# Reordering the normalisation and the stores at the end of a fused attention and FFN layer

## The chip, the cores and the metric

The kernel runs on one core of one Trainium2 chip. The metric is the device time of a run in microseconds (us). The core has a matrix engine (TensorE, "PE" in the profile, with its weight loads as "PEld"), a vector engine (VectorE, "DVE"), a scalar engine with function tables (ScalarE, "ACT"), a general engine (GpSimd, "POOL") and a queue engine (SyncE, "SP"). Each engine runs its own instructions in order; semaphores order them against each other. DMA transfers can be issued by SP, by ScalarE and by GpSimd.

## The reference

The input is `x`, 4 x 2048 tokens of 256 features in float32. Two sublayers follow each other, each with a residual and a layer norm:

```python
x = layernorm(x + attn(x))     # attn: S = (Q K^T) * decay mask, in chunks of 32 tokens; O = S V
                               # attn(x) = (sigmoid(x W_g^T) * O) W_o^T + x
x = layernorm(x + ffn(x))      # ffn: silu(x wg^T) * (x wu^T), times wd^T, hidden size 768
```

The FFN weights are integers from -127 to 127 with a scale of 1/127. `layernorm` subtracts the mean over the 256 features and divides by the root of variance + 1e-5; it has no gain and no bias.

## The kernel before, in words

The 8192 tokens are cut into 16 blocks of 512 (`TB`), and each block into four groups of 128 tokens (`NG`), one token per partition. A loop over `b` from 0 to 13 overlaps the FFN of block `b` with the attention of block `b + 2`; one iteration takes 32 us. Blocks 14 and 15 have their FFN after the loop, in the tail. Three products in the attention are done with seven multiplications instead of eight (`seven`), with sums made on GpSimd. The FFN multiplies activations split in a high part and an fp16 rest (`u_hi`, `u_lo`).

The program is written with a tile framework: it inserts the semaphores, hands out the buffers of each pool in turn (the eight PSUM banks by `bank`), and chooses the order of each engine's instructions from a planner's priorities and costs. An instruction may so run much earlier than it is written. Where `in_turn` (that is, `tc.keep_in_program_order`) is wrapped around an instruction, it keeps its written place among all instructions so wrapped.

The FFN keeps the integer weights exact only up to 128 in size. So the kernel looks at the weights' largest values (`look_up`, one piece at the end of each of the first six iterations, 0.94 us on VectorE), counts how many are too large (`count_wide`: a comparison `wide` on VectorE, a matmul of one row `pw`, a sum and a cast on VectorE to `n_wide`), and reads that count at the very end. If it isn't zero, everything is done again in float32 (`wide_block`); with these inputs it is zero, and the branch costs only the reading of `n_wide` on each engine (L929) and the jump (L932).

The tail is what the change is about. `ffn_up` (L646) multiplies up for block 15 in two halves of 256 tokens, `ffn_down` makes `r_before`, the residual of block 14, and `moments` (L290, `bn_stats` at L295 and `bn_aggr` at L296) its mean and variance in `mv_before`. After `count_wide` (L801), `root` (L299) has ScalarE take the square root `std_before`. That changes ScalarE's function table[...]. Then a loop over the four groups of block 15 does for each group `g`:

- 12 matmuls (L853) and the residual `r[:, g, :]` on VectorE (L861), then its moments (L295, L296);
- for `g == 0`, `normalize` of all of block 14: reciprocal (L806) and rescale (L809) on VectorE, four shifts, minus mean times reciprocal, on GpSimd (L815), four scalings on ScalarE (L824), and then one store of 512 KB from SP (L691);
- the root of this group on ScalarE (L304);
- for `g` 1 and 2, `normalize_first`: the oldest waiting group is normalised in the same way and stored, 128 KB from SP (L838). At `g == 2` it is called twice.

Group 3 is then normalised on VectorE alone (L876, L877) and stored. Because of `in_turn`, the reciprocal for a group stands in VectorE's order at the place where `normalize` is called.

Of the kernel before, what the change touches and what calls it, by code (L numbers as in the profile page):

```python
# [47 lines left out]
F32 = mybir.dt.float32  # L48
# [3 lines left out]
AF = mybir.ActivationFunctionType  # L52
ALU = mybir.AluOpType

P = 128
# [3 lines left out]
TB = 512  # L59
NG = TB // P  # L60
# [3 lines left out]
H_UP = 2.0**23  # L64
# [6 lines left out]
def kernel(  # L71
# [15 lines left out]
    nc = tc.nc  # L87
    NT, D = x.shape
# [1 line left out]
    KD = D // P  # L90
    KH = H // P
    NB = NT // TB
    assert NB > 3

    const = ctx.enter_context(tc.tile_pool(name="const", bufs=1))
    setup = ctx.enter_context(tc.tile_pool(name="setup", bufs=2))
# [1 line left out]
    work = ctx.enter_context(tc.tile_pool(name="work", bufs=2))  # L98
# [6 lines left out]
    small = ctx.enter_context(tc.tile_pool(name="small", bufs=8))  # L105
    psum = ctx.enter_context(tc.tile_pool(name="psum", bufs=8, space=bass.MemoryType.PSUM))

    def bank(name):
        return psum.tile([P, TB], F32, tag="ps", name=name)


    def span(b, start):
        return slice(b * TB, (b + 1) * TB) if start is None else bass.ds(start, TB)
# [142 lines left out]
    top = const.tile([P, 6], F32, tag="top", name="top")  # L256

    def look_up(i):
        w = (fg, fu, fd)[i // 2][0].bitcast(F32)
        half = w.shape[1] // 2  # L260
        reduced = nc.vector.tensor_reduce(
            top[:, i : i + 1],
            w[:, i % 2 * half : (i % 2 + 1) * half, :].rearrange("p k n -> p (k n)"),
            mybir.AxisListType.X,
            ALU.max,
            apply_absolute_value=True,
        )
        tc.keep_in_program_order(reduced)

    def count_wide():  # L270

        wide = const.tile([P, top.shape[1]], F32, tag="wide", name="wide")
        nc.vector.tensor_scalar(wide, top, EXACT, None, ALU.is_gt)
        ones = const.tile([P, 1], F32, tag="ones", name="ones")
        nc.vector.memset(ones, 1.0)
        pw = bank("pw")
        nc.tensor.matmul(pw[:1, : top.shape[1]], lhsT=ones, rhs=wide, start=True, stop=True)
        count = const.tile([1, 1], F32, tag="count", name="count")
        nc.vector.tensor_reduce(count, pw[:1, : top.shape[1]], mybir.AxisListType.X, ALU.add)
        n_wide = const.tile([1, 1], I32, tag="n_wide", name="n_wide")  # L280
        nc.vector.tensor_copy(n_wide, count)
        return n_wide

    def in_turn(ins):
        tc.keep_in_program_order(ins)
# [4 lines left out]
    def moments(r, name, groups=range(NG), order=free):  # L290

        mv = small.tile([P, NG, 2], F32, tag="mv", name=f"mv_{name}")
        for g in groups:
            st = small.tile([P, 6], F32, tag="st", name=f"st_{name}_{g}")
            order(nc.vector.bn_stats(st, r[:, g, :]))  # L295
            order(nc.vector.bn_aggr(mv[:, g, :], st))  # L296
        return mv

    def root(mv, name, on_r=1.0, groups=range(NG), order=free):  # L299

        std = small.tile([P, NG], F32, tag="rstd", name=f"rstd_{name}")
        span = slice(groups[0], groups[-1] + 1)
        order(
            nc.scalar.activation(  # L304
                std[:, span], mv[:, span, 1], AF.Sqrt, bias=eps, scale=1 / on_r**2
            )
        )
        return std
# [236 lines left out]
    def back_terms(g, parts, ws):  # L545


        pairs = list(zip(parts, ws))[:: -1 if g % 2 else 1]
        return [term for part, w in pairs for term in zip(part, w)]
# [128 lines left out]
    def ffn_down(b, uT, h):  # L678
        r = work.tile([P, NG, D], F32, tag="r2", name=f"r2_{b}")

        def residual(gs, pb):

            nc.vector.scalar_tensor_tensor(
                flat(r, gs), pb, SCALE**3 / U_UP * H_UP, flat(h, gs), ALU.mult, ALU.add
            )

        project_back(b, uT, [chunked(w) for w in fd], residual, "fdn")
        return r

    def store(b, r, start=None):  # L690
        nc.sync.dma_start(  # L691
            out[span(b, start), :].rearrange("(g p) d -> p g d", p=P), r
        )
# [38 lines left out]
    looked = 0  # L732

    for b in range(NB - 2):
# [38 lines left out]
        r = ffn_down(b, uT, hs.pop(b))  # L773
# [3 lines left out]
        if looked < top.shape[1]:  # L777
            look_up(looked)
            looked += 1
    for i in range(looked, top.shape[1]):  # L780
        look_up(i)

# [2 lines left out]
    last = NB - 1  # L787
    per = NG // 2
    cols = [slice(i * per * P, (i + 1) * per * P) for i in range(2)]
# [7 lines left out]
    r_before = ffn_down(last - 1, uT, hs[last - 1])  # L797
    mv_before = moments(r_before, f"f{last - 1}")
    ffn_up(last, hTs[last], uT_last, range(len(early), KH), cols[0])
    ffn_up(last, hTs[last], uT_last, range(KH), cols[1])  # L800
    n_wide = count_wide()  # L801

    def normalize(r, mv, rstd, name, on_r=1.0, groups=range(NG)):

        span = slice(groups[0], groups[-1] + 1)
        in_turn(nc.vector.reciprocal(rstd[:, span], rstd[:, span]))  # L806
        if on_r != 1:
            in_turn(
                nc.vector.tensor_scalar(  # L809
                    rstd[:, span], rstd[:, span], 1 / on_r, None, ALU.mult  # L810
                )
            )
        shift = small.tile([P, NG], F32, tag="shift", name=f"shift_{name}")
        for g in groups:
            nc.gpsimd.tensor_scalar(  # L815
                shift[:, g : g + 1],
                mv[:, g, 0:1],
                rstd[:, g : g + 1],
                -1.0,
                ALU.mult,  # L820
                ALU.mult,
            )
        for g in groups:
            scaled = nc.scalar.activation(  # L824
                r[:, g, :],
                r[:, g, :],
                AF.Identity,
                bias=shift[:, g : g + 1],
                scale=rstd[:, g : g + 1],
            )  # L830
            in_turn(scaled)

    std_before = root(mv_before, f"f{last - 1}", H_UP, order=in_turn)
    r = work.tile([P, NG, D], F32, tag="r2", name=f"r2_{last}")

    def store_group(g):
        tokens = slice(last * TB + g * P, last * TB + (g + 1) * P)
        nc.sync.dma_start(out[tokens, :], r[:, g, :])  # L838

    waiting = []

    def normalize_first():
        g, mv, std = waiting.pop(0)
        normalize(r, mv, std, f"f{last}_{g}", groups=[g])
        store_group(g)

    for g in range(NG):
        pb = bank(f"fdn_{last}_{g}")[:, :D]  # L850
        terms = back_terms(g, uT_last, map(chunked, fd))
        for i, (part, w) in enumerate(terms):
            nc.tensor.matmul(  # L853
                pb,
                lhsT=part[:, g * P : (g + 1) * P],
                rhs=w,
                start=(i == 0),
                stop=(i == len(terms) - 1),
            )
        in_turn(  # L860
            nc.vector.scalar_tensor_tensor(  # L861
                r[:, g, :], pb, SCALE**3 / U_UP, hs[last][:, g, :], ALU.mult, ALU.add
            )
        )
        mv = moments(r, f"f{last}_{g}", [g], order=in_turn)
        if g == 0:
            normalize(r_before, mv_before, std_before, f"f{last - 1}", H_UP)
            store(last - 1, r_before)
        std = root(mv, f"f{last}_{g}", groups=[g], order=in_turn)
        waiting.append((g, mv, std))  # L870
        if 0 < g < NG - 1:
            normalize_first()
        if g == NG - 2:
            normalize_first()
    g, mv, std = waiting.pop()
    in_turn(nc.vector.reciprocal(std[:, g : g + 1], std[:, g : g + 1]))  # L876
    nc.vector.tensor_scalar(  # L877
        r[:, g, :], r[:, g, :], mv[:, g, 0:1], std[:, g : g + 1], ALU.subtract, ALU.mult
    )
    store_group(g)  # L880


    def wide_block(start, weights):
# [46 lines left out]
        n_wide, min_val=0, max_val=top.shape[1] * P, skip_runtime_bounds_check_because="a count"  # L930
# [63 lines left out]
```

## Time and profile before

| | us |
|---|---|
| median of 3 runs | 536.26 (535.37 to 536.46) |
| the profiled execution's own time | 535.63 |
| its span | 533.9 |
| last matmul begins, last VectorE instruction ends | 524.1, 528.99 |
| last store issued | 529.3 |

The span is what the profile covers of the execution; the 1.73 us between it and the execution's own time lie around it. In the profile's rows, "128x256 f32<-128x256 f32 x4" are output and input shapes (partitions x elements) and the count; a bracket at a row's end tells how long the engine sat idle before it and which instruction released it. "L824" is a line of the kernel. All times in the tail are from the start of the span. The mean granted TensorE clock is 0.995.

### The profile page before, as it was taken

The page shows a single profiled execution, that of the slowest core. Times are in us where ns is not written, and L with a number is a line of the kernel's source. Part 1 is how long each engine was busy: PE and PEld are TensorE (multiplying, and loading weights), DVE is VectorE, ACT ScalarE, POOL GpSimd, SP SyncE. Part 2 cuts the span into 40 slices and gives each one's busy share as a digit, 9 for nine tenths or more (in the row PEclk, how much of TensorE's full clock was granted, in tenths as well). Part 3 has the DMA queues.
Part 4 walks back from the last instruction along what each step waited for, and adds up shares of the span by engine and source line. Part 5 has one row for each costly group of instructions (what it writes and reads, how often), then busy time and mean ns, then how long its engine had stood idle before and what let it go on. Part 6 is the DMA issues. An engine that isn't in the chain of part 4 may idle for free.

```text
span 533.9 us, 9939 instructions
## 1 busy us (share of the span) xinstructions
PE 522.8 (98%) x3486; PEld 421.0 (79%) x3486; DVE 391.2 (73%) x1026; ACT 310.8 (58%) x561; POOL 268.4 (50%) x305
## 2 busy tenths in 40 slices
PE   8999999999999999999999999999999999999992
PEld 5688887888878788887888878788887888868792
DVE  4468659587695867859587695867859587698883
ACT  2284556555564754656555664764657566566754
POOL 5132672735636365572735636374572736433651
PEclk9999999999999999999999999999999999999997
DMA  7531312214130231412214130231412113020102
GB/s 253 181 120 39 80 40 69 52 41 119 42 101 18 52 108 41 114 46 63 58 39 120 41 105 15 54 107 40 112 49 78 42 43 78 1 65 16 40 2 82
DMA packets 43126, 36.87 MB, mean 69 GB/s; under 512 B 4673, under 2 KB 38977, under 8 KB 43073
## 3 DMA queue, kind: packets, MB, share of 16 engines
q1 hardware_dynamic: 41952, 35.15, 23.3%
q10 hardware_dynamic: 1088, 1.05, 0.6%
q8 instruction: 29, 0.48, 0.4%
q14 instruction: 25, 0.20, 0.1%
q0 software_dynamic: 32, 0.00, 0.0%
HBM read 20.45 MB, written 8.39 MB: 54 GB/s over the span
## 4 chain that ended last, share of the span: by engine, by line
PE 95%; DVE 2%; ACT 1%; issue 0%; DVEq 0%; POOL 0%
PE fg L656 16%; PE fdn L561 16%; PE fu L656 15%; PE pa L561 10%; PE p_v L379 8%; PE p_y L363 8%; PE p_g L363 8%; PE po L535 5%; PE ps L514 3%; PE pg L459 1%; PE py L475 1%; PE pv L494 1%; PE pi L177 1%; DVE u L668 1%; DVE s L666 1%
## 5 line engine op out<-in xcount | busy, mean ns | idle before, releaser
L676 POOL TENSOR_TENSOR u_lo<-u,u_hi 128x512 f16<-128x512 f32 (+1 forms) x102 | 123.7, 1214 | 144.3 <-ACT u_hi L675 143.8
L666 DVE SCALAR_TENSOR_TENSOR s<-fg,s 128x512 f32<-128x512 f32 (+1 forms) x102 | 66.4, 651 | 48.1 <-ACT s L664 47.6
L664 ACT ACTIVATE s<-fg 128x512 f32<-128x512 f32 (+1 forms) x102 | 58.2, 571 | 66.6 <-PE fg L656 65.9
L675 ACT CAST u_hi<-u 128x512 fp32r<-128x512 f32 (+1 forms) x102 | 60.4, 592 | 31.5 <-DVE u L668 30.7
L656 PE MATMUL fg<-hT_hi,fg_hi 128*128 128x512 f32 (+1 forms) x204 | 74.0, 443 | 0.0
L668 DVE TENSOR_TENSOR u<-fu,s 128x512 f32<-128x512 f32 (+1 forms) x102 | 66.1, 650 | 5.0 <-POOL u_lo L676 1.0
L656 PE MATMUL fu<-hT_hi,fu_hi 128*128 128x512 f32 (+1 forms) x204 | 61.6, 382 | 0.0
L656 PE MATMUL fg<-hT_lo,fg_lo 128*128 128x512 f16 (+1 forms) x204 | 58.9, 370 | 0.0
L656 PE MATMUL fu<-hT_lo,fu_lo 128*128 128x512 f16 (+1 forms) x204 | 58.1, 366 | 0.0
L561 PE MATMUL pa<-wo,goT 128*128 128x256 f32 x256 | 58.0, 379 | 0.0
L561 PE MATMUL fdn<-fd_hi,u_hi 128*128 128x256 f32 x360 | 55.4, 296 | 0.0
L561 PEld LDWEIGHTS pa<-wo,goT 128*128 128x128 f32 x256 | 48.6, 190 | 6.7
L640 POOL TENSOR_TENSOR hT_lo<-hT,hT_hi 128x512 f16<-128x512 f32 x28 | 35.4, 1286 | 28.5 <-ACT hT_hi L639 28.5
L561 PEld LDWEIGHTS fdn<-fd_hi,u_hi 128*128 128x128 f32 x360 | 46.8, 189 | 1.1
L561 PE MATMUL fdn<-fd_lo,u_lo 128*128 128x256 f16 x360 | 44.7, 274 | 0.0
L656 PEld LDWEIGHTS fu<-hT_hi,fu_hi 128*128 128x128 f32 x204 | 37.5, 188 | 7.7
L656 PEld LDWEIGHTS fg<-hT_hi,fg_hi 128*128 128x128 f32 x204 | 35.7, 189 | 8.5
L304 ACT ACT_TABLE_LOAD x30 | 38.5, 1283 | 0.5
L656 PEld LDWEIGHTS <-fu_lo 128*128 128x128 f16 x204 | 20.0, 98 | 21.5 <-DVE sT L524 1.2
L561 PEld LDWEIGHTS <-u_lo 128*128 128x128 f16 x360 | 32.7, 98 | 5.1 <-POOL u_lo L676 0.3
L582 DVE SCALAR_TENSOR_TENSOR h<-x,pa 128x512 f32<-128x512 f32 x32 | 22.0, 688 | 17.5 <-PE pa L561 16.9
L535 PE MATMUL po<-sT,v 128*128 128x128 f32 x256 | 31.2, 275 | 0.0
(150 smaller groups left out, 983.7 us busy)
## 6 DMA issues: line engine op xcount, KB each, us to landing
x<-in_x_dram SPq DMA_DIRECT2D x16, 512.0 KB, 3.4
xT<-in_xT_dram SPq DMA_DIRECT2D x15, 512.0 KB, 4.4
out_dram<-r SPq DMA_DIRECT2D x15, 512.0 KB, 5.1
hT<-sq SPq DMA_DIRECT2D x224, 32.0 KB, 1.9
fg_int<-in_ffn_gT_dram SPq DMA_DIRECT2D x3, 256.0 KB, 8.1
fu_int<-in_ffn_uT_dram SPq DMA_DIRECT2D x3, 256.0 KB, 6.5
fd_int<-in_ffn_dT_dram SPq DMA_DIRECT2D x3, 256.0 KB, 6.0
xT<-in_xT_dram SPq DMA_DIRECT2D x2, 256.0 KB, 3.8
```

Source lines behind the costliest of these rows:

```text
L304: nc.scalar.activation(std[:, span], mv[:, span, 1], AF.Sqrt, bias=eps, scale=1 / on_r**2)
L363: nc.tensor.matmul(pb, lhsT=a[i - 1], rhs=b[i - 1], start=first, stop=True, skip_group_check=True,)
L379: nc.tensor.matmul(pb[:, g * P : (g + 1) * P], lhsT=b[i - 1][:, g * P : (g + 1) * P], rhs=a[i - 1], start=first and g == 0, stop=True, ski ...
L535: nc.tensor.matmul(po[:, cols], lhsT=v[:, g, dc * P : (dc + 1) * P], rhs=sT[:, cols], start=True, stop=True,)
L561: nc.tensor.matmul(pb[:, j * D : (j + 1) * D], lhsT=part[:, g * P : (g + 1) * P], rhs=w, start=(i == 0), stop=(i == len(terms) - 1),)
L640: nc.gpsimd.tensor_tensor(in_order[1], whole, in_order[0].bitcast(F32), ALU.subtract)
L656: nc.tensor.matmul(pb, lhsT=w[kind][:, dc, hc * P : (hc + 1) * P], rhs=hT[kind][:, dc, cols], start=(kind == kinds[0] and dc == 0), stop=( ...
L664: nc.scalar.activation(s, pg, AF.Sigmoid, scale=SCALE / H_UP)
L666: nc.vector.scalar_tensor_tensor(s, pg, U_UP / H_UP**2, s, ALU.mult, ALU.mult)
L668: nc.vector.tensor_tensor(u, pu, s, ALU.mult)
L675: nc.scalar.copy(hi, u)
L676: nc.gpsimd.tensor_tensor(lo, u, hi.bitcast(F32), ALU.subtract)
```

## The change

What is scaled where, and in which order it is stored, changes in the tail:

- `count_wide` is called in iteration 6 of the loop instead of in the tail.
- The reciprocals of block 14 and of group 0 of block 15 stand behind the moments of group 1; those of group 1 behind the moments of group 2; those of groups 2 and 3 at the end.
- Block 14: groups 0 and 1 are scaled by ScalarE, 2 and 3 by GpSimd. Its four shifts become one product for all groups (`shift_before`), with minus the mean computed ahead (`minus_mean`). Four stores of 128 KB take the place of the one of 512 KB: groups 0 and 2 from SP, 1 and 3 from ScalarE's queue.
- Block 15: groups 0 and 1 are scaled by ScalarE (shift 0 on GpSimd, shift 1 on VectorE), groups 2 and 3 by VectorE.
- Stores are in turn as well.

```diff
         if looked < top.shape[1]:
             look_up(looked)
             looked += 1
-    for i in range(looked, top.shape[1]):
-        look_up(i)
+        elif looked == b:
+            n_wide = count_wide()
...
-    n_wide = count_wide()
...
+    def inverse(std, cols, on_r=1.0):
+        in_turn(nc.vector.reciprocal(std[:, cols], std[:, cols]))
         if on_r != 1:
...
+                nc.vector.tensor_scalar(std[:, cols], std[:, cols], 1 / on_r, None, ALU.mult)
...
+    def by_vector(eng, r, g, mv, std):
+
+        in_turn(
+            eng.tensor_scalar(
                 r[:, g, :],
                 r[:, g, :],
+                mv[:, g, 0:1],
+                std[:, g : g + 1],
+                ALU.subtract,
+                ALU.mult,
+            )
+        )
+
+    def by_scalar(r, g, std, shift):
+        scaled = nc.scalar.activation(
+            r[:, g, :], r[:, g, :], AF.Identity, bias=shift, scale=std[:, g : g + 1]
+        )
+        in_turn(scaled)
+
+    def shift_of(eng, g, mv, std):
+        shift = small.tile([P, 1], F32, tag="shift_last", name=f"shift_{last}_{g}")
+        in_turn(
+            eng.tensor_scalar(
+                shift, mv[:, g, 0:1], std[:, g : g + 1], -1.0, ALU.mult, ALU.mult
+            )
+        )
+        return shift
...
+    minus_mean = small.tile([P, NG], F32, tag="minus", name=f"minus_{before}")
+    nc.vector.tensor_scalar(minus_mean, mv_before[:, :, 0], -1.0, None, ALU.mult)
+    shift_before = small.tile([P, NG], F32, tag="minus", name=f"shift_{before}")
+    of_group = []
     for g in range(NG):
...
         mv = moments(r, f"f{last}_{g}", [g], order=in_turn)
         if g == 0:
-            normalize(r_before, mv_before, std_before, f"f{last - 1}", H_UP)
-            store(last - 1, r_before)
-        std = root(mv, f"f{last}_{g}", groups=[g], order=in_turn)
-        waiting.append((g, mv, std))
-        if 0 < g < NG - 1:
-            normalize_first()
-        if g == NG - 2:
-            normalize_first()
...
+            std_before = root(mv_before, f"f{before}", H_UP, order=in_turn)
+        of_group.append((mv, root(mv, f"f{last}_{g}", groups=[g], order=in_turn)))
+        if g == 1:
+            inverse(std_before, slice(0, NG), H_UP)
+            mv, std = of_group[0]
+            inverse(std, slice(0, 1))
+            shift = shift_of(nc.gpsimd, 0, mv, std)
+            in_turn(
+                nc.gpsimd.tensor_tensor(shift_before, minus_mean, std_before, ALU.mult)
+            )
+            by_scalar(r, 0, std, shift)
+            store_group(last, r, 0)
+            for g_before in (2, 3):
+                by_vector(nc.gpsimd, r_before, g_before, mv_before, std_before)
+            by_scalar(r_before, 0, std_before, shift_before[:, 0:1])
+            for g_before in (0, 2):
+                store_group(last - 1, r_before, g_before)
+        if g == 2:
+            mv, std = of_group[1]
+            inverse(std, slice(1, 2))
+            by_scalar(r, 1, std, shift_of(nc.vector, 1, mv, std))
+            store_group(last, r, 1)
+    by_scalar(r_before, 1, std_before, shift_before[:, 1:2])
+    for g in (2, 3):
+        mv, std = of_group[g]
+        inverse(std, slice(g, g + 1))
+        by_vector(nc.vector, r, g, mv, std)
+        store_group(last, r, g)
+    for g in (1, 3):
+        store_group(last - 1, r_before, g, nc.scalar)
```

More of the change, by code (lines that the diff above doesn't have):

```diff
@@ L92 @@
     NB = NT // TB
-    assert NB > 3
+    assert NB > 9
     const = ctx.enter_context(tc.tile_pool(name="const", bufs=1))
@@ L800, with store_group @@
     ffn_up(last, hTs[last], uT_last, range(KH), cols[1])
-    n_wide = count_wide()
-    def normalize(r, mv, rstd, name, on_r=1.0, groups=range(NG)):
-        span = slice(groups[0], groups[-1] + 1)
-        in_turn(nc.vector.reciprocal(rstd[:, span], rstd[:, span]))
+    r = work.tile([P, NG, D], F32, tag="r2", name=f"r2_{last}")
+    def store_group(b, r, g, eng=nc.sync):
+        tokens = slice(b * TB + g * P, b * TB + (g + 1) * P)
+        in_turn(eng.dma_start(out[tokens, :], r[:, g, :]))
@@ L807, in normalize @@
+    def inverse(std, cols, on_r=1.0):
+        in_turn(nc.vector.reciprocal(std[:, cols], std[:, cols]))
         if on_r != 1:
             in_turn(
-                nc.vector.tensor_scalar(
-                    rstd[:, span], rstd[:, span], 1 / on_r, None, ALU.mult
-                )
-            )
[L813 to L816, printed above, removed]
+                nc.vector.tensor_scalar(std[:, cols], std[:, cols], 1 / on_r, None, ALU.mult)
+            )
@@ L817, in normalize @@
+    def by_vector(eng, r, g, mv, std):
+        in_turn(
+            eng.tensor_scalar(
+                r[:, g, :],
+                r[:, g, :],
                 mv[:, g, 0:1],
-                rstd[:, g : g + 1],
-                -1.0,
-                ALU.mult,
+                std[:, g : g + 1],
+                ALU.subtract,
                 ALU.mult,
             )
[L823 to L829, printed above, removed]
-            )
-            in_turn(scaled)
@@ L833 @@
[L833 to L847, printed above, removed]
+        )
[4 more added lines that the diff above has]
+        in_turn(scaled)
@@ new lines, in shift_of @@
+    def shift_of(eng, g, mv, std):
[3 more added lines that the diff above has]
+                shift, mv[:, g, 0:1], std[:, g : g + 1], -1.0, ALU.mult, ALU.mult
+            )
+        )
+        return shift
+    before = f"{last - 1}"
+    minus_mean = small.tile([P, NG], F32, tag="minus", name=f"minus_{before}")
+    nc.vector.tensor_scalar(minus_mean, mv_before[:, :, 0], -1.0, None, ALU.mult)
+    shift_before = small.tile([P, NG], F32, tag="minus", name=f"shift_{before}")
@@ L866 @@
         if g == 0:
-            normalize(r_before, mv_before, std_before, f"f{last - 1}", H_UP)
-            store(last - 1, r_before)
-        std = root(mv, f"f{last}_{g}", groups=[g], order=in_turn)
-        waiting.append((g, mv, std))
-        if 0 < g < NG - 1:
-            normalize_first()
-        if g == NG - 2:
-            normalize_first()
[L875 to L880, printed above, removed]
+            std_before = root(mv_before, f"f{before}", H_UP, order=in_turn)
[28 more added lines that the diff above has]
+        store_group(last - 1, r_before, g, nc.scalar)
     def wide_block(start, weights):
```

## The prediction

> **What bounds the kernel now.** The page comes first: over the span TensorE is the bound, and it can't be shortened by this change.
>
> ```profile
> span 533.9 us, 9939 instructions
> PE 522.8 (98%) x3486; PEld 421.0 (79%) x3486; DVE 391.2 (73%) x1026; ACT 310.8 (58%) x561; POOL 268.4 (50%) x305
> ```
>
> But the edit lies in the last 15 us, so I read the stage, not the share. The windows view (length, busy time and count of PE, PEld, DVE, ACT, POOL, then granted clock, DMA share, GB/s) shows that TensorE is done by 524.3 and that no engine computes in the last five microseconds:
>
> ```profile
> 520.62:524.32 3.70, 3.70 (x33) 3.34 (x30) 1.97 (x8) 2.87 (x5) 1.71 (x5) 1.00 0.02 4
> 524.32:528.99 4.67, 0.01 (x1) 0.00 (x0) 2.82 (x11) 3.43 (x9) 0.79 (x3) 0.94 0.51 169
> 528.99:533.90 4.91, 0.00 (x0) 0.00 (x0) 0.00 (x0) 0.00 (x0) 0.00 (x0) 0.50 0.19 60
> ```
>
> The timeline (start, length) says why 4.7 us pass between the last matmul and the last vector instruction:
>
> ```profile
> 521.91 0.30 ACT L304 ACTIVATE rstd_f<-mv_f,eps 128x4 f32<-128x4 f32 x1
> 523.03 2.07 ACT L824 ACTIVATE r<-r,shift_f,rstd_f 128x256 f32<-128x256 f32 x4 [0.82 <-POOL shift_f L815]
> 525.01 0.47 ACT L304 ACTIVATE rstd_f<-mv_f,eps 128x1 f32<-128x1 f32 x2
> 525.32 0.16 DVE L806 RECIPROCAL rstd_f<-rstd_f 128x1 f32<-128x1 f32 x1 [1.69 <-ACT rstd_f L304]
> 525.40 0.41 DVE L861 SCALAR_TENSOR_TENSOR r<-fdn,h 128x256 f32<-128x256 f32 x1
> 528.58 0.41 DVE L877 TENSOR_SCALAR r<-r,mv_f,rstd_f 128x256 f32<-128x256 f32 x1
> 526.50 3.23 SPq L838 DMA_DIRECT2D out_dram<-r  x4
> ```
>
> ScalarE scales all four groups of block 14 (2.07 us) before it takes the roots of groups 0 and 1 of block 15. The reciprocal of group 0 stands in VectorE's order ahead of the residual of group 2, whose matmuls ended by 523; so VectorE idles 1.69 us. Then two more groups of residual, statistics, root, reciprocal and scaling follow, and four stores. The last store is issued at 529.3 and lands 2.7 later (the stores' own view), at 532.0; the span ends 1.9 after that.
>
> ```profile
> L838 SPq DMA_DIRECT2D out_dram<-r x4: 345/401/1143, 526.5 to 529.3; - x4
> DMA to landing us min/median/max: 2.6/2.7/3.5
> ```
>
> [...] Here issuing takes 0.35 to 0.49 us against 2.6 and more to land[...]. [...] this one, begun beside a 1.28 us GpSimd subtraction (487.32 to 489.97, two of them), took 1372 ns where the median is 403.
>
> ```profile
> L319 DVE TENSOR_SCALAR h<-h,mv_a,rstd_a x4: 396/403/1372, 488.4 to 490.4; 128x256 f32<-128x256 f32 x4
> ```
>
> The residual (487.4) and bn_stats (488.1) beside the same subtractions kept their usual 0.69 and 0.43.
>
> **The change, part by part.**
>
> *count_wide moves from the tail to iteration 6.* Two matmuls of one pass, 0.12 us of TensorE, leave the tail and enter the loop: net nothing, so later absolute times stay. VectorE's reduce and cast (0.14 + 0.13) join it near 281, behind the scaling that ends at 281.2. Cover: iterations with a 0.94 us look-up at that very place last 32.0 us, as do those without. If that cover fails it costs what it delays; I allow 0.1 for the bank that `pw` holds from 275 to about 281.6, when the eighth bank after it is wanted (281.8). Bounds: 0 and 0.4. In the tail the 0.27 freed on VectorE lets residual 0 start at most 0.1 earlier; group 1's matmuls decide anyway.
>
> *Order on VectorE.* Residual 1 no longer waits behind the reciprocals for block 14: its matmuls end at 521.62 (last start 521.33 + 0.29), so it starts at 521.69 instead of 522.53. Then, with spacings read from groups 2 and 3 of before (residual to bn_stats 0.46, to bn_aggr 0.46, to reciprocal 0.10): bn_aggr ends 522.79, reciprocal and rescale of block 14 end 523.09, reciprocal 0 523.17. Its roots are there: table load to 521.90, roots to 522.40. Residual 2 starts 523.10, bn_aggr 2 ends 524.20, reciprocal 1 524.27, shift 1 (new on VectorE, priced as the 0.17 of the 128x4 tensor_scalar) 524.49. Residual 3 starts 524.45, bn_aggr 3 ends 525.55. The new `minus_mean`, 0.17, isn't held in order and has 8 us of VectorE gaps since 512.3; I charge nothing. If it were late it would cost its 0.17.
>
> *GpSimd.* Shift 0 523.27 to 523.54 (265 ns); `shift_before` for all four groups in one tensor_tensor, by 523.78 (priced as a shift). Two scalings follow. No row shows this one: 128x1 takes 265 ns, 128x128 with one operation 530, so 256 elements give 0.80 with the same slope and 1.33 with a doubled one; a tensor_tensor of the size takes 0.73. I take 1.05. GpSimd ends at 525.85 (525.4 to 526.4). Behind its first scaling SP's third store waits until 524.8, and behind that store SP's fourth, ready only at 525.36: nothing lost.
>
> *ScalarE.* Root 1 by 523.1; scaling of r group 0 523.59 to 524.18; of block 14 group 0 to 524.67; root 2 to 524.87; r group 1 524.77 to 525.36; root 3 behind bn_aggr 3, 525.60 to 525.89; block 14 group 1 to 526.38. It scales four groups where it did seven; GpSimd and VectorE have two each.
>
> *End on VectorE.* Reciprocal 2 at 525.47. Scaling 2 would start at 525.67 but excludes GpSimd's last one, so 525.95; reciprocal 3; scaling 3 ends about 526.7, against 528.99: 2.3 earlier.
>
> *Stores.* The one of 512 KB becomes four of 128, eight in all. SP issues six, about 0.4 each, from 524.25; the last (group 3) at about 526.8. ScalarE's queue issues block 14's groups 1 and 3 at 526.45 and, at the 0.49 of its early loads, 526.95; only ScalarE's exit is queued behind them. So the last issue moves from 529.3 to 526.95. Landing: 2.7 when alone, 3.5 seen behind a 512 KB store. Eight times 131 KB at the 340 GB/s of 526 to 528 is 3.1 us; with first data 0.87 after the first issue (as at 525.13 to 526.0) they are through by 528.6, near what the last issue allows. I take 2.8: landed at 529.75 instead of 532.0, which is 2.25 earlier. The exit of 1.9 stays.
>
> *Sum.* −2.25 + 0.1 = −2.15: span 531.75, that execution's own 535.63 becomes 533.5. The median of the runs shown, 536.26, lies 0.63 above that execution; from the median, 534.1.
>
> **Rivals.**
>
> *Stores crowd (0.14).* One of the four stores of before occupied SP for 1.14 us, with four in flight, and one took 3.5 to land. If the last two take these (issue +0.1, landing 3.5), the gain is 1.45, less 0.1 for the loop: 534.9. Against it: the eight are spread over 2.7 us, and the data rate above allows them.
>
> *GpSimd scaling dearer (0.14).* At 1.33 each GpSimd ends at 526.4, VectorE's two scalings wait for it, the last store issues at 527.35: gain 1.75, 534.5. At 1.6: last issue 527.9, gain 1.2, 535.1. [...] Only from 2.3 each would the gain be gone; nothing on the page is near that.
>
> *Slower: TensorE stalls in the loop (0.08).* TensorE is in order. If `wide`, which its matmuls read, ran at its written place behind iteration 6's scaling (281.2), they would hold TensorE from 275.1 to about 281.5: 6.4 lost on the bound, net +4.15, 540.4. It decides once `wide` ends after 277.3. Against it: `wide` ran at 253.6, four microseconds after the last look-up, though written at the end of the program; it will again.
>
> *It doesn't do what it says.* Block 14's groups 1 and 3 are not stored early but last; that is in the sum. The rest is an order written by hand, so this adds little.
>
> **How the numbers follow.** Forecast 0.64, own range 533.5 to 534.7 (landing 2.6 to 3.0, GpSimd 0.8 to 1.2, loop 0 to 0.4). About 0.2%, 1.07 us, is what a measurement of this kernel can tell from no change; before's runs spread as much. Faster by more (under 535.2): 0.64, about 0.09 of each of the first two rivals: 0.82. Same: 0.10. Slower: 0.08. The range 533.3 to 535.4 takes in both rivals.
>
> **What would show it.** Right: VectorE's wait of 1.69 gone; residual 1 near 521.7; the last scaling on VectorE ending by 526.7; last issue, on ScalarE's queue, near 527; 1.9 from landing to end. Wrong: GpSimd's 128x256 above 1.33 us with a VectorE scaling stretched beside it; a landing over 3.3; a PE wait near 275 or 281.8.

## The result, and the profile after

The kernel after takes 534.66 us (median of 12 runs, 534.2 to 535.0), the kernel before beside it 536.12 (12 runs, 535.32 to 536.54). The ratio is 0.9975, with a 95% interval from 0.9966 to 0.9984: 1.46 us faster. The forecast was 534.1. The profiled execution of the kernel after took 534.32 us, with this head of the page:

```profile
span 532.6 us, 9935 instructions
PE 522.2 (98%) x3486; PEld 420.4 (79%) x3486; DVE 392.3 (74%) x1029; ACT 308.8 (58%) x558; POOL 269.9 (51%) x302
```

TensorE is as busy as it was (522.2 us against 522.8), and its last matmul ends 0.28 us earlier (524.05, before 524.33); the rest of the gain lies behind it, in the tail. The windows view of the tail of after (same columns as in the prediction), cut at the last matmul and at the last vector instruction:

```profile
520.62:524.05 3.43, 3.43 (x30) 3.07 (x29) 2.93 (x13) 2.71 (x6) 1.74 (x4) 1.00 0.02 5
524.05:526.40 2.35, 0.01 (x1) 0.00 (x0) 2.21 (x8) 1.70 (x5) 1.69 (x2) 1.00 0.49 156
526.40:532.60 6.20, 0.00 (x0) 0.00 (x0) 0.00 (x1) 0.00 (x0) 0.00 (x0) 0.51 0.37 116
```

The middle stage shrank from 4.67 to 2.35 us, and VectorE is now busy for 2.21 of it: that is the reordering, and it did what it says. But the stage in which nothing computes grew from 4.91 to 6.20. More than half of what was won is lost behind the last instruction, and that is what the experiments are about. The timeline of after (start, length, and in brackets the idle time ahead and its releaser):

```profile
521.35 0.43 DVE L860 SCALAR_TENSOR_TENSOR r<-fdn,h 128x256 f32<-128x256 f32 x1 [0.25 <-PE fdn L852]
...
523.92 0.21 DVE L836 TENSOR_SCALAR shift<-mv_f,rstd_f 128x1 f32<-128x1 f32 x1
...
525.28 0.60 DVE L817 TENSOR_SCALAR r<-r,mv_f,rstd_f 128x256 f32<-128x256 f32 x1
525.81 0.14 DVE L808 RECIPROCAL rstd_f<-rstd_f 128x1 f32<-128x1 f32 x1
525.99 0.41 DVE L817 TENSOR_SCALAR r<-r,mv_f,rstd_f 128x256 f32<-128x256 f32 x1
```
```profile
523.30 2.44 POOL L817 TENSOR_SCALAR r<-r,mv_f,rstd_f 128x256 f32<-128x256 f32 x2
```

Residual 1 starts at 521.35, the wait of 1.69 us is gone, and VectorE ends at 526.40 instead of 528.99. GpSimd takes 1.22 us for one scaling, and VectorE's scaling of group 2, which begins beside GpSimd's second, takes 0.60 instead of 0.41. The stores' own view of after (durations of the issue in ns, first and last start) and the DMA view from 520 to 534 (its 40 slices of 0.35 us, then queues and issues):

```profile
L805 SPq DMA_DIRECT2D out_dram<-r x6: 351/402/803, 523.8 to 526.7; - x6
L805 ACTq DMA_DIRECT2D out_dram<-r x2: 405/436/467, 526.0 to 526.5; - x2
```
```profile
GB/s 0 0 0 0 0 0 0 0 0 0 47 0 23 181 176 18 307 240 234 366 313 340 307 322 138 32 32 23 23 15 0 0 0 0 0 0 0 0 0 0
...
q8 instruction: 2, 0.03, 1.2%
...
out_dram<-r SPq DMA_DIRECT2D x6, 128.0 KB, 3.0
out_dram<-r ACTq DMA_DIRECT2D x2, 128.0 KB, 3.9
```

The last store is issued at 526.7, before the 526.95 of the forecast. It lands 4.1 us later, at 530.8, where the forecast took 2.8. The GB/s row shows how: mostly above 300 from 525.6 to 528.4, one slice of 138, and then five of 15 to 32, about a sixteenth of the rate before (340 / 16 is 21). Each of the eight stores raises its semaphore in sixteen steps, and the page counts 16 DMA engines. I read a step as the part of the store that one engine carries; the trace doesn't name the engine of a step. Read so, the landing events tell whether all engines are late or one. Of the store issued last, fourteen had landed at 529.00, the fifteenth at 529.87, the sixteenth at 530.76. In the four stores before it the sixteenth came 1.8 to 2.0 us behind the fourteenth. From 529.4 to the end the packets in the trace come one at a time, 42 ns apart, eight of 1 KB for each store, which would fit a single engine that works off a backlog. (The late fifteenth part of the last store may belong to a second instruction queue, which moved 8 KB at 528.42; no run tested that.)

In that stretch the queue marked "instruction" moves two packets of 16 KB, at 523.50 (1.17 us long) and at 526.84 (1.49 us): by the queue's name, instructions fetched for an engine. The view of the conditional's line, L947, in after names whose (operation, count, duration in ns, start):

```profile
L947 PEldq COMPARE_BRANCH  x1: 3602/3602/3602, 522.5 to 522.5; - x1
L947 POOLq COMPARE_BRANCH  x1: 45/45/45, 523.4 to 523.4; - x1
...
L947 DVEq COMPARE_BRANCH  x1: 72/72/72, 526.6 to 526.6; - x1
...
L947 ACTq COMPARE_BRANCH  x1: 54/54/54, 527.8 to 527.8; - x1
L947 SPq COMPARE_BRANCH  x1: 45/45/45, 528.0 to 528.0; - x1
```

Four engines jump over the float32 fallback in 45 to 72 ns. TensorE, which jumps over some 425 instructions by a count of the program, needs 3.6 us, from 522.5 to 526.1. The second fetch begins 0.7 us after that. The kernel before has the same jump, 3.34 us long.

### The profile page after: what moved, and what is told of

Read it like the earlier page. It is cut to its first block, busy times and chain, and to the rows that moved or that the text cites. A ratio compares the mean times of both kernels' runs of the same rounds, so it can differ in the third digit from the quotient of the medians.

```text
span 532.6 us, 9935 instructions
## 1 busy us (share of the span) xinstructions
PE 522.2 (98%) x3486; PEld 420.4 (79%) x3486; DVE 392.3 (74%) x1029; ACT 308.8 (58%) x558; POOL 269.9 (51%) x302
## 4 chain that ended last, share of the span: by engine, by line
PE 93%; DVE 3%; DMA 1%; POOL 0%; issue 0%; ACT 0%; DVEq 0%
PE fg L656 16%; PE fu L656 15%; PE fdn L561 15%; PE pa L561 10%; PE p_v L379 8%; PE p_y L363 8%; PE p_g L363 8%; PE po L535 5%; PE ps L514 3%; PE py L475 1%; PE pg L459 1%; PE pv L494 1%; DMA wg<-in_w_gT_dram 1%; DVE u L668 1%; DVE st_f L295 1%; PE fdn L852 1%
```

## The experiments

**Theory.** TensorE's jump makes it fetch instructions, 16 KB at a time, through one of the sixteen DMA engines. That engine's part of every store issued about then is held until the fetch is through, and the last store with it. **Rival.** Eight stores of 128 KB from two queues crowd each other, as the prediction had feared.

**1 and 2. Both kernels without the conditional.** The whole of `wide_any` and its block are left out, so there is no fallback.

```diff
-    wide_any = nc.values_load(
-        n_wide, min_val=0, max_val=top.shape[1] * P, skip_runtime_bounds_check_because="a count"
-    )
-    with tc.If(wide_any > 0):
...
```

> The changed kernel without the reading of n_wide and without the branch and the float32 block behind it, which these inputs never enter (left out: the fallback for large weights; the count itself is still made). Fetch theory: the last stores land 4 us after issue because one of the 16 DMA engines is held by a 16 KB instruction fetch that TensorE's jump over that block sets off at 526.8. Without the jump there is no fetch there, and the last store lands 2.3 to 2.9 after its issue: span shorter than that of the changed kernel by 1.2 to 1.9 us (about 531.0), run time about 533.0. Crowding theory (eight stores from two queues): landing stays near 4, the span changes by less than 0.5.

> The kernel before with the same part left out, to pair with e1. Fetch theory: its last store waited 0.8 us on one DMA engine, so it gains 0.6 to 1.0 (span about 533.0), and the reordering is then worth e2 minus e1 = 1.9 to 2.4 us. Crowding theory: it gains nothing, and e2 minus e1 stays near the measured 1.5.

Measured: after without it 532.26 us (ratio to before 0.9932, interval 0.9919 to 0.9946); before without it 534.37 (0.9967, 0.9955 to 0.9979). In the first the stores and their issues are those of after; the tail's DMA view of it:

```profile
GB/s 0 0 0 0 0 0 0 0 0 0 0 0 0 0 0 3 310 231 234 322 258 155 313 354 334 342 141 0 0 0 0 0 23 0 0 0 0 0 0 0
...
out_dram<-r SPq DMA_DIRECT2D x6, 128.0 KB, 1.8
out_dram<-r ACTq DMA_DIRECT2D x2, 128.0 KB, 2.1
```

The same eight stores at the same rate land in 1.7 to 2.3 us, with no trickle behind: the sixteenth part of the last store comes 0.04 us after the fourteenth. So crowding is not what held the stores of after for 4 us. A little of it seems to be there: the last four stores are issued within 0.54 us and land about 0.37 us apart, and the last one takes 2.32, where the last of before without the conditional takes 1.69.

Between these two kernels the change is worth 534.37 − 532.26 = 2.11 us in medians, and 1.82 in means, give or take 0.6 with five and six runs. That is near the 2.15 of the prediction's sum, but doesn't tell it from the 1.46 measured with the conditional. The two traces show the parts, counted from the end of the last matmul: the last issue comes 2.27 us earlier (2.40 for 4.67), the last landing 1.64 earlier (4.72 for 6.36); the difference is the longer landing. The conditional costs the kernel before about 1.4 us (535.73 beside it, − 534.37), the kernel after about 2.4 (534.66, on another occasion, − 532.26), its reading included.

**3 and 4. Where the code lies, and one queue.** Number 3 puts eight matmuls of one column at TensorE's start, to shift all its instructions; number 4 issues all stores from SP.

```diff
+    for _ in range(8):
+        nc.tensor.matmul(pi[:1, :1], lhsT=idle[:, :1], rhs=idle[:, :1], start=True, stop=True)
```
```diff
-        store_group(last - 1, r_before, g, nc.scalar)
+        store_group(last - 1, r_before, g)
```

> The changed kernel with eight one-column matmuls (16 passes, 32 TensorE instructions) added behind the warm-up at the start, where TensorE waits for weights anyway. [...] Fetch theory: the fetches near the end fall at another time; [...] the last store lands below 3.3 us and the run is 0.7 to 1.6 us shorter; if the fetch still falls between 525 and 529, nothing changes, but it has moved. Crowding theory: no change of the time and of the landing, wherever the fetch falls.

> The changed kernel with block 14's groups 1 and 3 stored from SP too, behind group 3 of block 15. Fetch theory: landing stays near 4 for the stores behind the fetch; the last issue is later by one or two issues (0.4 to 0.8 us), and the span longer by 0.3 to 0.8, as the late DMA engine hides part of it. Crowding theory, with the second queue at fault: landing falls below 3.3 and the span is shorter by up to 0.7.

Measured: 534.83 (0.9985, 0.9978 to 0.9992) and 534.71 (0.9979, 0.9969 to 0.9988). The padding left the jump (3.78 us) and both fetches in place and told nothing. With one queue, the last issue begins 0.8 us later than in after (527.5), and yet the last part lands at 530.89 against 530.76: the time of the last issue did not decide. That issue itself took 1366 ns here.

**5 and 6. More padding, and GpSimd left out.** Number 5 splits the warm-up matmuls in eight each, for 56 more instructions on TensorE. Number 6 has ScalarE scale groups 1 to 3 of block 14, and its queue store them.

```diff
-    for _ in range(WARM):
-        nc.tensor.matmul(pi, lhsT=idle[:, :P], rhs=idle, start=True, stop=True)
+    for i in range(8 * WARM):
+        cols = slice(i % 8 * 64, (i % 8 + 1) * 64)
+        nc.tensor.matmul(
+            pi[:32, cols], lhsT=idle[:, :32], rhs=idle[:, cols], start=True, stop=True
+        )
```
```diff
-            for g_before in (2, 3):
-                by_vector(nc.gpsimd, r_before, g_before, mv_before, std_before)
...
-    by_scalar(r_before, 1, std_before, shift_before[:, 1:2])
+    for g in (1, 2, 3):
+        by_scalar(r_before, g, std_before, shift_before[:, g : g + 1])
```

> The changed kernel with the two warm-up matmuls of 512 columns at the start cut into sixteen of 64 columns (the same columns on 32 weight columns; only idle zeros are multiplied): 56 more TensorE instructions ahead of everything. [...] Fetch theory: with 56 more, [...] the wait at TensorE's branch (3.4 to 3.8 us) falls below 2, the second fetch starts before 525.5, and the last store lands 2.0 to 3.2 us after issue; run time 533.0 to 534.2 against the changed kernel's 534.7. If the count is off, the fetches stay where they are relative to the stores and the time stays within 0.4 of the changed kernel's. Crowding theory: landing stays near 4 wherever the fetch is.

> The changed kernel with block 14's groups 2 and 3 scaled by ScalarE behind group 1, and stored from its queue, so that GpSimd scales nothing. Lock theory: VectorE's scaling of group 2, 0.60 us beside GpSimd's, falls back to 0.41, and VectorE is done 0.2 earlier; ScalarE's last scaling ends 1.0 later (about 527.0) and its last issue is at about 528.0 instead of 526.5. Fetch theory: the late DMA engine hides much of that: run time 0 to 0.8 above the changed kernel. If GpSimd were the hidden cost of the change, it would be faster by 0.3 or more.

Measured: 534.42 (0.9976, 0.9969 to 0.9984) and 534.34 (0.9975, 0.9966 to 0.9985). Padding didn't keep the fetch away: jump 3.66 us, fetches at 523.54 and 527.25, last landing 530.81. The idea that a lucky place of the code would avoid it fell. In number 6 VectorE's scaling of group 2 is short again:

```profile
525.59 0.41 DVE L817 TENSOR_SCALAR r<-r,mv_f,rstd_f 128x256 f32<-128x256 f32 x1
```

So 0.60 in after was GpSimd's doing. The last issue is at 527.3, 0.7 later than in after, and the last landing at 530.87: once more the same time.

**7. The kernel before, with block 14's normalisation moved behind group 1.** Nothing else of the change is taken over.

```diff
-        if g == 0:
-            normalize(r_before, mv_before, std_before, f"f{last - 1}", H_UP)
-            store(last - 1, r_before)
...
+        if g == 1:
+            normalize(r_before, mv_before, std_before, f"f{last - 1}", H_UP)
+            store(last - 1, r_before)
```

> The kernel before with one edit: block 14 is normalised (all of it by ScalarE, one store, as before) behind group 1's root instead of behind group 0's moments. Order theory: residual 1 starts near 521.7 and VectorE's 1.69 us wait shrinks, but root 2 now stands behind five scalings on ScalarE, so VectorE waits for it before residual 3: its last scaling ends about 528.5 against 528.99, run time 0.2 to 0.8 below the kernel before. If the order alone made the gain, it would be 1.4 or more below.

Measured: 535.46 us, ratio 0.9998 (0.9990 to 1.0006), no gain that can be told; the interval leaves room for 0.5 us. The timeline:

```profile
521.24 0.42 DVE L861 SCALAR_TENSOR_TENSOR r<-fdn,h 128x256 f32<-128x256 f32 x1 [0.25 <-PE fdn L853]
...
523.01 2.57 ACT L824 ACTIVATE r<-r,shift_f,rstd_f 128x256 f32<-128x256 f32 x5 [0.34 <-POOL shift_f L815]
...
525.49 0.28 ACT L304 ACTIVATE rstd_f<-mv_f,eps 128x1 f32<-128x1 f32 x1
...
525.80 0.16 DVE L806 RECIPROCAL rstd_f<-rstd_f 128x1 f32<-128x1 f32 x1 [2.02 <-ACT rstd_f L304]
```

Residual 1 is early, but ScalarE scales five groups in a row ahead of group 2's root, and VectorE now waits 2.02 us at that group's reciprocal. Still its last scaling ends at 527.93, 1.06 earlier than before. Then the stores take 3.3 to 4.7 us to land, their sixteenth parts 0.6 to 1.9 behind the fourteenth beside a fetch at 528.11, and the last is down at 531.23 (before: 531.93).

**8. The count put back in the tail of after.**

```diff
-        elif looked == b:
-            n_wide = count_wide()
...
+    n_wide = count_wide()
```

> The changed kernel with count_wide called in the tail, where the kernel before has it. Forecast's sum: the 0.2 us of TensorE that it takes leave the loop and enter the tail, VectorE's 0.25 with them: run time within 0.3 of the changed kernel, either way. If the move carries part of the gain, it is 0.5 or more slower.

Measured: 534.57 (0.9976, 0.9970 to 0.9982), as after. The move of `count_wide` carries no part that can be seen.

**9, 10, 11 and 12. The jump moved, the jump made short, and after again.** In number 9 one matmul that reads the last scaled group stands ahead of TensorE's jump; in number 10 it reads group 1 (`r[:, 1, 0:1]`). In number 11 the conditional stays, on every engine, but the loop over the float32 block is taken out of it.

```diff
+    pd = bank("late_jump")[:1, :1]
+    nc.tensor.matmul(pd, lhsT=r[:, NG - 1, 0:1], rhs=r[:, NG - 1, 0:1], start=True, stop=True)
```
```diff
-        with tc.For_i(0, NT, TB) as start:
-            wide_block(start, weights)
+        pd = bank("short_block")[:1, :1]
+        w = weights[0][0]
+        nc.tensor.matmul(pd, lhsT=w[:, 0, 0:1], rhs=w[:, 0, 0:1], start=True, stop=True)
```

> The kernel after, with one float32 matmul of one column added on TensorE, which reads the last scaled group of block 15 (its scaling ends at 526.4), ahead of TensorE's reading of the count and its jump. So the jump starts some 4 us later than the 522.5 of the kernel after, and the two 16 KB fetches start near 527.6 and 531 instead of 523.5 and 526.8. Theory (the fetch holds one of the 16 DMA engines and with it the last stores): the first fetch now falls into the stores' landing (526.7 to 529.0) and holds it by about its own length, 1.2 to 1.5 us, so the last landing stays near 530.5 and the time at the kernel after's or, because TensorE's jump itself now ends at about 530.3, slightly above: 534.3 to 535.2. If instead the lag comes with two fetches together, or only with the second, the landing falls to about 529.3 and the time to 533.4. If the stores lag from crowding alone, the landing stays at 530.8 and no store's lag moves with the fetch.

> The kernel after, with one float32 matmul of one column added on TensorE ahead of its reading of the count and its jump, which reads group 1 of block 15, scaled by about 525.0, so TensorE's jump starts near 525.2 and the fetches near 526.2 and 529.5. Theory: the first fetch is through at about 527.6 and the last stores, issued to 526.7, are held by less, while the second comes after 529.3, when the stores are down: last landing 529.3 to 530.0, time 533.2 to 534.0, 0.5 to 1.3 below the kernel after. If the first fetch holds the stores as the second did in the kernel after: no gain, 534.6. Crowding: no change, 534.6, with the lag at the same stores.

> The kernel after with the conditional kept (count, reading, comparison and jump on every engine) but the loop over the float32 block left out of it, so that what TensorE jumps over is one matmul in place of some 425 instructions; the output has no fallback. If the fetch of TensorE's code behind the jump is what delays the last stores: no 16 KB fetch between 523 and 530, TensorE's jump lasts well under 1 us, all 16 DMA engines land within 0.3 us of each other, landing at most 2.5 us, last landing near 529.0 and a time of 532.3 to 532.8 as without the conditional. If reading the count and jumping cost the time themselves, whatever the distance: 534.6 as the kernel after. Between the two, the rest over 532.3 is the price of the conditional on the other engines.

> The kernel after unchanged, run beside the three kernels with a moved or a short jump: 534.2 to 535.0, 0.9970 to 0.9985 of the kernel before, with the last store landing about 4 us after its issue and one DMA engine behind the other fifteen.

Measured, with the times in the profiled executions (us; the head of an execution differs by up to 1.3 us, so the interval from the end of the last residual matmul to the last landing is the one to compare):

| kernel | time | ratio to before, interval | TensorE's jump | 16 KB fetches | sixteenth behind fourteenth part, last store | last matmul to last landing |
|---|---|---|---|---|---|---|
| before | 535.91 | | 522.8 to 526.1 | 523.80, 527.84 | 0.82 | 7.60 |
| after again (12) | 534.27 | 0.9971, 0.9960 to 0.9981 | 522.6 to 526.3 | 523.60, 527.09 | 0.71 | 6.93 |
| jump late (9) | 534.45 | 0.9972, 0.9962 to 0.9981 | 527.4 to 531.5 | 528.58, 532.19 | 0.44 | 5.15 |
| jump mid (10) | 534.38 | 0.9972, 0.9961 to 0.9983 | 527.1 to 530.9 | 528.11, 531.61 | 1.41 | 6.12 |
| short block (11) | 532.89 | 0.9945, 0.9931 to 0.9958 | 223 ns | none | 0.05 | 4.94 |

In the row of before, the time is that of its runs beside these four kernels, and the rest is from the trace that the prediction read. In number 12 the last store's issue took 2.08 us, so that even its fourteenth part was late, at 530.37; hence the 0.71. The four stores before it show 1.9 to 2.1.

In number 11 the conditional is read and jumped on every engine, but the jump is short, no 16 KB fetch is seen, the stores land in 1.7 to 2.1 us and 1.4 us of time are gone (534.27 − 532.89):

```profile
L947 SPq COMPARE_BRANCH  x1: 45/45/45, 498.0 to 498.0; - x1
...
L947 PEldq COMPARE_BRANCH  x1: 223/223/223, 522.8 to 522.8; - x1
```
```profile
out_dram<-r SPq DMA_DIRECT2D x6, 128.0 KB, 1.7
out_dram<-r ACTq DMA_DIRECT2D x2, 128.0 KB, 1.9
```

So a conditional as such doesn't cost the 1.4 us. But this kernel is not after with a shorter jump alone: the block is short on every engine, the 8 KB fetches beside the stores are gone too, and the framework moved the reading and the jump forward, on SP to 498.0 and on VectorE to 524.1, ahead of residual 2, where they hold it up:

```profile
524.48 0.43 DVE L860 SCALAR_TENSOR_TENSOR r<-fdn,h 128x256 f32<-128x256 f32 x1 [0.74 <-DVEq L947]
```

That wait may be part of the 0.6 us by which number 11 is slower than number 1 in medians; the two were measured on different occasions, and their intervals overlap.

Number 9 singles TensorE out, because there only TensorE's jump has moved, and with it the fetch. The fetch begins at 528.58, when the stores are nearly down, and the last lands at 529.35, 1.4 us earlier than in after, though the other engines read and jump as they did there, and 8 KB fetches fall where they did (528.70, in after 528.42). Together, 1, 9 and 11 show that the late landing goes with TensorE's long jump. I had expected 530.5, since the fetch came 1 us later than I had placed it. But the time is that of after, because the end now waits for TensorE itself: SP sits 1.52 us in one wait, from 530.07, that ends behind TensorE's semaphore (views of the conditional's line and of the stores):

```profile
L949 PEldq COMPARE_BRANCH  x1: 4038/4038/4038, 527.4 to 527.4; - x1
...
L949 PEldq EVENT_SEMAPHORE  x1: 51/51/51, 531.5 to 531.5; - x1
```
```profile
L805 SPq DMA_DIRECT2D out_dram<-r x6: 332/348/401, 524.0 to 526.6; - x6
L805 ACTq DMA_DIRECT2D out_dram<-r x2: 374/412/450, 526.2 to 526.6; - x2
...
DMA to landing us min/median/max: 1.8/1.9/2.7
```

Number 10 was expected to gain 0.5 to 1.3 us and gained nothing. Its tail ran 1.3 us late in the profile, its first fetch fell at 528.11 to 529.40, amid the last stores, and one part of each of the last four came 1.4 to 1.7 us behind the fourteenth, as beside the second fetch in after. So of the three places tried for the jump none costs less than the others.

None of the kernels that keep the fallback is faster than after by more than the measurement can tell. Those that beat it, 1 and 11, leave the fallback out.

## Why the prediction was right, and where it was off

**The reordering: right.** Residual 1 was forecast for 521.69 and came at 521.35, the last scaling on VectorE to end about 526.7 and it ended at 526.40, the last issue at 526.95 and it came at 526.7. Some 0.3 of that is a tail that began earlier: the last residual matmul ended at 524.05 instead of 524.33. Experiments 1 and 2 give the whole reordering 2.11 us in medians (1.82 in means, give or take 0.6) where no fetch is in the way, against 2.15 in the sum; the last issue they bring forward by 2.27, against 2.35.

**GpSimd's scaling: too cheap, inside its bounds.** Taken at 1.05, measured at 1.22 (bounds 0.80 and 1.33). VectorE's scaling was placed behind GpSimd's last one; it began beside it and was stretched by 0.19. It ended 0.15 behind GpSimd's last one (525.74 to 525.88), and so did the scaling of 1372 ns that the prediction showed (489.97 to 490.12): both were stretched beside a GpSimd instruction (0.60 for 0.41, 1.37 for 0.40), but the full 0.41 didn't follow behind it, as the prediction's exclusion had it. Neither decided anything: experiment 6 takes GpSimd out, and the time stays.

**The last queue: wrong, without a price.** The last issue comes from SP, not from ScalarE's queue: ScalarE's two went out at 526.05 and 526.5.

**The landing: the term that was mis-sized.** The sum took 2.8 us from the last issue to landing; it was 4.1. The last landing moved from 531.93 to 530.76, by 1.17, not by 2.25. With 1.8 us from landing to end, where 1.95 had been, the span fell to 532.6, not to 531.75: the landing is 1.3 too long, the last issue 0.3 early, the end 0.1 short, and the 0.1 allowed for the loop did not show. In the profiled executions the forecast so missed by 0.8 us (534.32 for 533.5), in the medians by 0.56; the gain was 1.46 for 2.15. Without the fetch, 2.8 would even have been too long: in number 1 the stores land in 1.7 to 2.3. One sum on the way there was off too, without weight: 524.25 + 0.87 + 3.1 is 528.2, not 528.6.

**Right in part by luck.** The landing of 4.1 lies outside the 2.6 to 3.0 of the forecast's own range, and above the 3.3 that the prediction had named as a sign of being wrong. The time still fell into 533.5 to 534.7, by 0.04, because the last issue came early, the end was short, and the kernel before ran at 536.12 instead of the 536.26 from which the forecast was counted.

**The stores-crowd rival: its number near, its mechanism wrong.** It gave 534.9 with a landing of 3.5. The stores do land late, but experiments 1, 9 and 11 land the same eight in at most 2.7 us. Data rate and number of stores, on which the argument turned, account for at most some 0.6 us of the last landing (experiments 1 and 2), not for the 4.1. The 1.14 us issue and the 3.5 us landing on which the rival rested were read from stores of before that went beside its own fetch: of the one that took 3.53, fourteen parts were down after 1.90.

**What the prediction didn't look at.** The description of the kernel called the conditional's cost the reading of the count and a jump. The trace of before had what was needed: a jump of 3.3 us on TensorE, 16 KB packets on the instruction queue at 523.80 and 527.84, and a rate of 12 GB/s in the last slices. The landing of 2.7 us read there was itself held up beside that fetch, its sixteenth part 0.82 us behind the fourteenth, and I took it for a property of a store. A compare-and-branch took 45 to 72 ns there on four engines and 3342 on TensorE; over one matmul it took TensorE 223 (number 11). With the long jump went two fetches of 16 KB, with the short one none; no run varied the length between 1 and some 425 instructions, and the shifts by padding in 3 and 5 changed nothing.

**The loop and the slower rival: right.** `pw` ran on TensorE at 274.8, the reduce at 276.1 and the cast at 276.9, with no stall of 6 us. Experiment 8 finds nothing for the move in either direction.

**Left open.** That the sixteen steps of a store are the parts of sixteen engines, and that the straggling one is on the engine that carries the fetch, is inferred from the counts, the times and the packets that come one at a time, as the trace doesn't name the engines; 1, 9 and 11 show the cause, not this detail. Nor does the fetch's own length give the lag: in number 4 the sixteenth part came 2.4 us late beside a fetch of 0.96. What the long jump waits for in its 3.3 to 4.0 us, when a fetch itself lasts 0.9 to 1.7, wasn't found. It isn't known either whether and how a fetch lengthens the issue of a store: the traces show the two together (the last section), and no run tested it.

## What to carry to other kernels

Before pricing a landing by a row of the profile, look at what it consists of. Here the rate fell from over 300 GB/s to 15 to 32 for the end of the landing, and in four stores the sixteenth part came 1.8 to 2.0 us behind the fourteenth; so the last issue came 2.6 us earlier than before (526.7 for 529.3), the last landing only 1.17. Read the end of the program on every engine's queue, jumps and instruction fetches among them, also on engines that have finished computing. A conditional block that hardly ever runs had a price here: on TensorE a jump of 3.6 us over some 425 instructions, 0.22 over one, paid where the jump falls. A shorter block, such as a loop with a smaller body, is worth trying where stores end the program; no run here tried one that still does the work.

## What the runs showed of the hardware

- A jump on TensorE over some 425 instructions took 3.3 to 4.0 us in the eleven profiles that have it; over one matmul, 0.22 (number 11).
- An instruction fetch of 16 KB took 0.9 to 1.7 us. Beside one, the last sixteenth of a store came up to 2.4 us behind the fourteenth (number 4); without one, stores of 128 KB landed in 1.7 to 2.3 us (1, 2 and 11).
- On GpSimd a tensor_scalar of 128x256 with two operands by pointer took 1.22 us, where one of 128x1 took 0.26 (after). VectorE's scaling beside it took 0.60, alone 0.41.
- Issues of stores in the tail took 0.33 to 0.47 us each in the five kernels without a 16 KB fetch among them (1, 2, 9, 10, 11; in 9 and 10 the first fetch begins after the last issue has begun). In the nine with one (before, after, 3 to 8, 12) the longest issue of each took 0.75 to 2.35 us.
- The table load on ScalarE ahead of block 14's root took 1.28 us (before, at 520.62; after, at 520.41).
- TensorE's jump, written behind a matmul that waits for the last scaled group, began at 527.4 us, where it began at 522.5 without it (number 9, after): it didn't overtake the matmul.
